# Attention and experts in fp32: products apart, sin from PSUM, other slots for the projections

## The chip, the cores and the metric

The kernel runs on one core of a Trainium2 chip. The metric is the device time of one execution in microseconds (us). A core has five engines that run their own instruction streams and meet through semaphores: TensorE (PE, with its weight loads shown apart as PEld), VectorE (DVE), ScalarE (ACT), GpSimd (POOL) and SyncE (SP), which here mostly issues DMA transfers. All arithmetic is fp32. SBUF holds tiles with 128 partitions; matmuls write to PSUM, from which DVE and ACT read.

## The reference

The input x is 4 batches x 1024 tokens x 256. Two layers follow one another, each with a residual and a layer norm:

```python
# attention, per batch: 16 heads of 64
proj = x @ W_in.T + b_in                  # q, k, v
q = rope(q, sin, cos); k = rope(k, sin, cos)
att = softmax(causal(q @ k.T / sqrt(64)))
x1 = layernorm(x + (att @ v) @ W_out.T + b_out)
# experts, 4096 tokens, 16 experts, the best 3 per token
gate = top3(softmax(x1 @ gate_w)); gate /= sum(gate)
x2 = layernorm(x1 + sum_e gate_e * (relu(x1 @ W1_e + b1_e) @ W2_e + b2_e))
```

with

```python
def _rope(x, sin, cos):
    d = x.shape[-1] // 2
    x_hi, x_lo = (x[..., :d], x[..., d:])
    y_lo = x_lo * cos + x_hi * sin
    y_hi = x_hi * cos - x_lo * sin
    return jnp.concatenate([y_lo, y_hi], axis=-1)
```

So a rotated tile is (tile x sin) + (tile with its halves swapped x cos), with the signs in the tables.

## The kernel before

**Pairs and slots.** Two heads of 64 fill the 128 partitions. The attention is a loop over 4 x 8 = 32 such pairs n (L428); b is the batch and p the pair in it. The 1024 queries of a pair are 8 chunks of 128. A pair has six slots k (L432) that take the chunks 7, 6, 5, 4, then 3 and 2 together, then 1 and 0 together. Chunk qc needs the (qc+1) x 128 keys up to the diagonal.

**What a slot does.** `scores` (L279) runs the score matmuls of the slot's chunks, at most 512 keys at a time, for both heads (L300). DVE adds the mask, copies the scores (negated by the factor of Q, -1/8) to SBUF and takes the running minimum in one instruction (L308, tile `nmax`), ACT takes the exponential and its sum (L320), `divide` (L331) forms the reciprocal on DVE (L334, `rinv`) and multiplies on POOL (L337). Two slots later `turn` (L346) transposes the probabilities P in blocks of 32 x 32 on DVE (L357), into `t_first` for the key half h = 0 (keys 0 to 511) and `t_last` for h = 1. `product` (L364) of key chunk j multiplies the turned P with the values `vr` on PE, 32 small matmuls on 32 x 64 array tiles (L378; the profile counts 64 instructions) into four PSUM tiles `y_ps`. It runs j = 7 first, j = 0 last; `close` (L386) then copies the four tiles to `yT` on ACT, and `out` (L397) multiplies `yT` with the output weights (L400, tile `oo`), a quarter in each of four slots; DVE adds it to the sum of the batch (L455, `acc`).

**Feeding the next pairs.** `project` (L200) makes half of Q or K of pair n+1: four matmuls into PSUM (L214, `pp`), an eviction on ACT with bias, and the scale for Q (L218). Once a tile of Q (512 wide) or K (1024 wide) is whole, four DMAs on SP copy it with its 32-row halves swapped (L230, `swq`, `swk`). `rotate` (L232) multiplies the tile in place by sin (L236; Q on DVE, K on POOL), the swapped copy by cos on POOL (L242), and adds on POOL (L245). `values` (L247) makes a quarter of V for two pairs at once (L254, `vv`), sends it to DRAM (`v_d`), and `spread` (L271) reads it back in the layout that the products need (`vr`).

**What sets the order.** PE runs in program order (L427). The other engines' order is set by a scheduler, to which `after(i, kind)` (L327) says that instruction i is issued after the last one of that kind. Matmul results of scores, projections, values and `out` share four PSUM buffers of the pool `ps_s`, the products four of `ps_y`. In slots k = 0 to 5 PE's order before is, with S, P, O, J, V for scores, product, out, projection and values:

| slot | before |
|---|---|
| 0 | S7, P4, O, J(K0) |
| 1 | S6, P3, P2, J(K1) |
| 2 | P1, P0, S5, J(Q1) |
| 3 | S4, P7, O, J(Q0) |
| 4 | S3, S2, P6, O, V |
| 5 | S1, S0, P5, O, V |

P4 to P0 belong to the pair before, P7 to P5 to the pair itself; J to the next pair. K is rotated at slot 2, Q1 (the queries 512 to 1023, which S7 to S4 need) at slot 3, Q0 at slot 5.

**Extra work in some pairs.** When a batch is done, its layer norm and router run among the pairs of the next batch: steps on DVE and PE in the slots 3 and 5 of pair p = 1, 1 and 3 of p = 2, the places of the entries at slot 3 of p = 3, and four indirect scatters on POOL (L673) in the slots 1 and 3 of p = 4, 5 and 6. In p = 7 POOL adds the output bias twice (L179, `residual`). The pairs p = 1, 2, 3 are called R1, R2, R3 below, those with scatters scatter pairs, and those without either plain. The experts come after the last pair.

Of the kernel before, what the change touches and what calls it, by code (L numbers as in the profile page):

```python
# [29 lines left out]
FP = mybir.dt.float32  # L30
# [7 lines left out]
P = 128  # L38
# [50 lines left out]
def attention(  # L89
# [5 lines left out]
    with ExitStack() as ctx:  # L95
# [54 lines left out]
        bq_s = cp.tile([P, NP], FP, tag="bq_s")  # L150
# [8 lines left out]
        nc.vector.tensor_scalar_mul(bq_s, bqk[:, 0, :], SCALE)  # L159
        mask = cp.tile([P, 512], FP, tag="mask")  # L160
        nc.gpsimd.memset(mask[:, : 512 - P], 0.0)
        make_causal_mask(nc, mask[:, 512 - P :], BIG)
# [35 lines left out]
        swps = {}  # L198

        def project(n, i, g):  # L200

            b, p = divmod(n, NP)
            if i == 0:
                res = rot[n, 0, g] = qkp.tile([P, 512], FP, tag=f"rotq{g}", name="rotq")
                half, whole = res, True
            else:
                whole = (n, 1) in rot
                if not whole:
                    rot[n, 1] = qkp.tile([P, T], FP, tag="rotk", name="rotk")
                res = rot[n, 1]  # L210
                half = res[:, ts(g, 512)]
            ps = ps_s.tile([P, 512], FP, tag="s", name="pp")
            for c in range(DC):
                nc.tensor.matmul(  # L214
                    ps, lhsT=wqk[n][:, c, i, :], rhs=xts[b, g][:, c, :],
                    start=(c == 0), stop=(c == DC - 1),
                )
            nc.scalar.activation(  # L218
                half, ps, AF.Identity,
                bias=(bq_s if i == 0 else bqk[:, 1, :])[:, p : p + 1],  # L220
                scale=SCALE if i == 0 else 1.0,
            )
            if whole:

                if i == 0:
                    swp = swps[n, 0, g] = qkp.tile([P, 512], FP, tag="swq", name="swq")
                else:
                    swp = swps[n, 1] = qkp.tile([P, T], FP, tag="swk", name="swk", bufs=1)
                for r in range(4):
                    nc.sync.dma_start(out=swp[ts(r, 32), :], in_=res[ts(r ^ 1, 32), :])  # L230

        def rotate(n, i, g=None):  # L232
            key = (n, i) if i else (n, i, g)
            swp, res = swps.pop(key), rot[key]
            at = slice(None) if i else ts(g, 512)
            first = (nc.gpsimd if i and n else nc.vector).tensor_tensor(  # L236
                res, res, sin[:, at], ALU.mult
            )
            if n:
                after(first, "divide" if i else "turn" if "turn" in order else "scores")  # L240
            eng = nc.vector if n == 0 and i else nc.gpsimd
            second = eng.tensor_tensor(swp, swp, cos[:, at], ALU.mult)  # L242
            if n:
                after(second, "divide")
            eng.tensor_tensor(res, res, swp, ALU.add)  # L245

        def values(n, cc):  # L247

            b = n // NP
            v = vp.tile([P, 2, 2, P], FP, tag="v", name="v")  # L250
            ps = ps_s.tile([P, 2, 2 * P], FP, tag="s", name="vv")
            for u in range(2):
                for c in range(DC):
                    nc.tensor.matmul(  # L254
                        ps[:, u, :],
                        lhsT=xts[b, cc // 2][:, c, ts(cc % 2 * 2 + u, P)], rhs=wv[n][:, c, :],
                        start=(c == 0), stop=(c == DC - 1),
                    )
            nc.scalar.copy(v.rearrange("p i u d -> p u i d"), ps.rearrange("p u (i d) -> p u i d", i=2))
            if cc == 0:  # L260
                vds[n // 2] = v_d.tile([NG, 2, 32, 2, 4, 2 * P], FP, tag="v_d", name="v_d")

            for i in range(2):
                nc.sync.dma_start(
                    out=vds[n // 2][cc // 2, i, :, cc % 2].rearrange("q k d -> k q d"),
                    in_=v[:, i],
                )
# [11 lines left out]
        def scores(n, qcs):  # L279
# [25 lines left out]
            for qc, hh, k0, n_k, s in parts:  # L305
                last = k0 + n_k == (qc + 1) * P
                m = sp.tile([P, 1], FP, tag=f"nmax{hh}", name="nmax")
                order["scores"] = nc.vector.tensor_tensor_reduce(  # L308
                    out=probs[n, qc, hh][:, ds(k0, n_k)], in0=s[:, :n_k],
                    in1=mask[:, 512 - n_k :] if last else zero[:, :n_k], scale=1.0,  # L310
# [3 lines left out]
                nmax[qc, hh] = m  # L314
                if last:
# [15 lines left out]
        def divide(n, ends, kind):  # L331
            for qc, rsum in ends:
                rinv = sp.tile([P, 2], FP, tag="rinv", name="rinv")
                after(nc.vector.reciprocal(rinv, rsum), kind)  # L334
# [11 lines left out]
        def turn(n, i, hh, kind):  # L346
# [5 lines left out]
            pr = probs.pop((n, i, hh))  # L352
            for h, (t, step) in enumerate(zip(turned[n], (7, 3))):
                n_j = min(4, i + 1 - 4 * h)
                if n_j <= 0:
                    continue
                order["turn"] = router.on_dve = after(nc.vector.transpose(  # L357
                    t[:, hh, :, ds(i - 4 * h, n_j, step=step), :],
                    pr[:, ds(512 * h, n_j * P)].rearrange("p (j u q) -> p u j q", u=4, q=32),
                ), kind)  # L360
# [48 lines left out]

        chunks = [(7,), (6,), (5,), (4,), (3, 2), (1, 0)]  # L410
        n_slots = len(chunks)
        n_pairs = B * NP
        for i, g in ((1, 0), (0, 0), (1, 1), (0, 1)):
            project(0, i, g)
        for cc in range(4):
            values(0, cc)
        rotate(0, 1)
        for g in (1, 0):
            rotate(0, 0, g)
# [7 lines left out]
        with tc.manual_schedule(engines={mybir.EngineType.PE}):  # L427
            for n in range(n_pairs + 2):  # L428
# [3 lines left out]
                for k in range(n_slots):  # L432
                    m, js = (n - 1, ((4,), (3, 2), (1, 0))[k]) if k < 3 else (n, (10 - k,))
                    if k == 2 and one_of(m):
                        for j in js:
                            product(m, j)
                        close(m)

                    ends = scores(n, chunks[k]) if one_of(n) else []
                    if k != 2 and one_of(m):  # L440
                        for j in js:
                            product(m, j)
                    part = None
                    if k in (0, 3, 4, 5) and one_of(n - 1 - (k == 0)):
                        part = out(n - 1 - (k == 0), (k - 3) % 4 if k else 3)
                    m, kk = divmod(n * n_slots + k - 2, n_slots)
                    last = "scores"
                    for hh in range(2):
                        if one_of(m):
                            for qc in chunks[kk]:  # L450
                                turn(m, qc, hh, last)
                            last = "turn"
                        if hh == 0 and part:
# [15 lines left out]
                    if one_of(n + 1):  # L469
                        if k < 4:  # L470
                            project(n + 1, *((1, 0), (1, 1), (0, 1), (0, 0))[k])
                        if k == 2:
                            rotate(n + 1, 1)
                        elif k in (3, 5):
                            rotate(n + 1, 0, int(k == 3))
                    m = n + 2 - n % 2
                    if k in (4, 5) and one_of(m):
                        values(m, 2 * (n % 2) + k - 4)
# [627 lines left out]
```

## Time and profile before

| | |
|---|---|
| median of 14 runs | 1807.1 us (1800.67 to 1810.48) |
| profiled execution | 1811.8 us, span 1809.9 |
| attention | to about 1345 us |
| busy share of the span PE, DVE, ACT, POOL | 89%, 64%, 39%, 66% |
| mean granted clock of PE | 0.96 of full speed |
| waits of PE for `nmax` at `oo` | 31.6 us, 24 times |
| waits of PE for `t_last` at products | 19.3 us, 11 times |
| waits of PE for the router's `x2T` | 17.6 us, 3 times |
| idle of PE ahead of products put down to "issue" | 14.3 us, 20 times |

A line of a timeline gives start, duration, engine, line of the code, operation, output and inputs, how many instructions it joins, and in brackets how long the engine was idle before and what ended that. A line of the list of waits gives who waited for whom, the total in us, how many times, and the longest. A line of a table of stretches gives the stretch, its length, the busy time of PE, PEld, DVE, ACT and POOL with the number of instructions, the granted clock as a fraction of full speed, the share of the DMA engines and their GB/s.

### The profile page before, as it was taken

How to read it: one execution, taken by the hardware profiler on the slowest of the kernel's cores; microseconds unless marked ns; L12 is line 12 of the kernel's file. 1: busy time of each engine (PE TensorE's matmuls, PEld its weight loads, DVE VectorE, ACT ScalarE, POOL GpSimd, SP SyncE). 2: the span in 40 equal slices, each digit the busy share in tenths (PEclk: the TensorE clock that was granted, in tenths of full speed). 3: DMA queues.
4: the chain of work that ended last, by engine and by line, in shares of the span. 5: the costliest groups of instructions: out<-in, count | busy, mean ns of one | idle time of the engine just before them, and what ended most of it. 6: DMA issues, size and time to landing. Idle time of an engine off the chain costs nothing.

```text
span 1809.9 us, 51958 instructions
## 1 busy us (share of the span) xinstructions
PE 1606.1 (89%) x20920; PEld 1120.3 (62%) x20920; DVE 1164.3 (64%) x3458; ACT 713.2 (39%) x1634; POOL 1192.0 (66%) x1077
## 2 busy tenths in 40 slices
PE   7899999988999899888999988898889999999980
PEld 3556555655555555555555555555568888888870
DVE  4588778877877679687877868867846222222224
ACT  3445444444444445343444544344422222222214
POOL 3777657755578856556888555577766778888542
PEclk9899999999999999999999989999899999999995
DMA  6364644564355545435455463343467989998747
GB/s 182 96 161 121 147 111 112 132 182 105 92 124 121 121 111 162 125 91 122 121 123 124 111 191 92 91 109 94 114 254 199 208 242 246 241 241 240 212 87 279
DMA packets 118167, 272.97 MB, mean 151 GB/s; under 512 B 21873, under 2 KB 72433, under 8 KB 102562
## 3 DMA queue, kind: packets, MB, share of 16 engines
q1 hardware_dynamic: 93122, 239.91, 48.5%
q0 software_dynamic: 24656, 29.68, 9.0%
q8 instruction: 167, 2.74, 0.7%
q14 instruction: 78, 0.64, 0.1%
q10 hardware_dynamic: 144, 0.01, 0.0%
HBM read 183.17 MB, written 52.79 MB: 130 GB/s over the span
## 4 chain that ended last, share of the span: by engine, by line
PE 59%; DVE 16%; DMA 9%; issue 8%; SPq 4%; ACT 3%; POOL 1%; ACTq 0%; DVEq 0%; POOLq 0%
PE y_ps L378 14%; PE ps L874 11%; PE ps L890 10%; PE s L300 8%; PE pp L214 6%; PE oo L400 4%; DVE p L308 4%; PE vv L254 4%; DMA swq<-rotq 3%; SPq L230 3%; DVE t_first L357 3%; DVE t_last L357 2%; ACT p L320 2%; DMA xT<-in_xT_dram 1%; PE ps L862 1%
## 5 line engine op out<-in xcount | busy, mean ns | idle before, releaser
L337 POOL TENSOR_SCALAR p<-p,rinv 128x512 f32<-128x512 f32 (+7 forms) x512 | 385.8, 769 | 405.8 <-DVE rinv L334 401.7
L320 ACT ACTIVATE p<-p,nmax 128x512 f32<-128x512 f32 (+7 forms) x512 | 392.0, 766 | 470.9 <-DVE nmax L308 411.7
L300 PE MATMUL s<-rotk,rotq 64*128 64x512 f32 (+3 forms) x1536 | 336.7, 522 | 46.0 <-DVE x2T L578 17.6
L300 PEld LDWEIGHTS s<-rotk,rotq 64*128 64x128 f32 x1536 | 158.5, 189 | 229.3 <-issue 96.6
L308 DVE CUSTOM_DVE_ANT_0 p<-s,zero 128x512 f32<-128x512 f32 x256 | 165.7, 684 | 206.1 <-PE s L300 206.1
L357 DVE STREAM_TRANSPOSE t_first<-p 128x512 f32<-128x512 f32 (+3 forms) x512 | 289.0, 588 | 1.0 <-POOL p L337 0.9
L214 PE MATMUL pp<-xT,wqk 128*128 128x512 f32 x512 | 253.2, 619 | 19.6 <-DVE nmax L308 10.6
L904 POOL DMA_INDIRECT sums<-y,ids x112 | 178.9, 1597 | 69.4 <-DVE y L900 38.5
L378 PE MATMUL y_ps<-t_first,vr 32*64 32x160 f32 (+3 forms) x8192 | 208.4, 339 | 13.6 <-issue 12.3
L879 ACT ACTIVATE hid<-ps,w 128x256 f32<-128x256 f32 x224 | 94.1, 471 | 314.4 <-issue 252.1
L895 DVE TENSOR_TENSOR y<-ps,w 128x512 f32<-128x512 f32 x56 | 38.7, 692 | 275.7 <-PE ps L890 275.7
L378 PEld LDWEIGHTS y_ps<-t_first,vr 32*64 32x64 f32 x8192 | 169.3, 131 | 66.2 <-issue 37.4
L874 PE MATMUL ps<-xg,w 128*128 128x256 f32 x896 | 204.4, 382 | 2.6 <-DVE xg L864 2.6
L890 PE MATMUL ps<-w,hid 128*128 128x256 f32 x896 | 202.6, 379 | 0.0
L890 PEld LDWEIGHTS ps<-w,hid 128*128 128x128 f32 x896 | 169.8, 190 | 23.0
L400 PE MATMUL oo<-wo,yT 128*128 128x256 f32 x512 | 153.0, 425 | 32.9 <-DVE nmax L308 31.6
L874 PEld LDWEIGHTS ps<-xg,w 128*128 128x128 f32 x896 | 167.1, 191 | 23.7 <-DVE xg L864 2.8
L378 PE MATMUL y_ps<-t_last,vr 32*64 32x96 f32 (+3 forms) x7424 | 146.3, 255 | 31.8 <-DVE t_last L357 19.3
L378 PEld LDWEIGHTS y_ps<-t_last,vr 32*64 32x64 f32 x7424 | 115.6, 135 | 92.9 <-issue 46.2
L214 PEld LDWEIGHTS pp<-xT,wqk 128*128 128x128 f32 x512 | 93.9, 194 | 111.4 <-issue 69.7
L308 DVE CUSTOM_DVE_ANT_0 p<-s,mask,nmax 128x512 f32<-128x512 f32 (+3 forms) x256 | 130.3, 545 | 0.8 <-issue 0.4
L400 PEld LDWEIGHTS oo<-wo,yT 128*128 128x128 f32 x512 | 91.6, 199 | 56.1 <-DVE nmax L308 35.2
(150 smaller groups left out, 2011.6 us busy)
## 6 DMA issues: line engine op xcount, KB each, us to landing
vr<-v_d SPq DMA_DIRECT2D x256, 256.0 KB
w<-in_wall_dram SPq DMA_DIRECT2D x56, 1154.0 KB
swq<-rotq SPq DMA_DIRECT2D x256, 64.0 KB
swk<-rotk SPq DMA_DIRECT2D x128, 128.0 KB
v_d<-v SPq DMA_DIRECT2D x128, 128.0 KB
wqk<-in_w_qk_dram SPq DMA_DIRECT2D x32, 256.0 KB
xT<-in_xT_dram SPq DMA_DIRECT2D x8, 512.0 KB
wv<-in_w_v_dram SPq DMA_DIRECT2D x16, 256.0 KB
```

The source lines that it names most:

```text
L214: nc.tensor.matmul(ps, lhsT=wqk[n][:, c, i, :], rhs=xts[b, g][:, c, :], start=(c == 0), stop=(c == DC - 1),)
L300: nc.tensor.matmul(s[:, :n_k], lhsT=rot[n, 0, qc // 4][ts(hh, KD), ts(qc % 4, P)], rhs=k[ts(hh, KD), ds(k0, n_k)], start=True, stop=True,)
L308: order["scores"] = nc.vector.tensor_tensor_reduce(out=probs[n, qc, hh][:, ds(k0, n_k)], in0=s[:, :n_k], in1=mask[:, 512 - n_k :] if last ...
L320: nc.scalar.activation(pr, pr, AF.Exp, bias=m, scale=-1.0, accum_out=rsum[:, hh : hh + 1])
L337: order["divide"] = router.behind = nc.gpsimd.tensor_scalar(pr, pr, rinv[:, hh : hh + 1], 1.0, ALU.mult, ALU.mult)
L357: order["turn"] = router.on_dve = after(nc.vector.transpose(t[:, hh, :, ds(i - 4 * h, n_j, step=step), :], pr[:, ds(512 * h, n_j * P)].rea ...
L378: nc.tensor.matmul(st[n][a][ts(hh, KD), ds(32 * j, 32 * (TC - j))], lhsT=vrs[n, h][ts(a, 32), jh // 2 * 8 + 2 * u + jh % 2, ts(hh, KD)], r ...
L400: nc.tensor.matmul(ps[:, v, :], lhsT=st[n][:, ts(2 * h + v, P)], rhs=wo[n], start=True, stop=True,)
L874: nc.tensor.matmul(ps[:, f - f0, :], lhsT=w[:, ds(c * FF + f * P, P)], rhs=xg[:, c, :], start=(c == 0), stop=(c == DC - 1),)
L879: nc.scalar.activation(hid[:, f, :], ps[:, f - f0, :], AF.Relu, bias=w[:, ds(B1_AT + f, 1)])
L890: nc.tensor.matmul(ps[:, h, :], lhsT=hid[:, f, ts(h, P)], rhs=w[:, ds(W2_AT + f * D, D)], start=(f == 0), stop=(f == FC - 1),)
L904: s = behind(nc.gpsimd.indirect_dma_start(out=sums[t % 2], out_offset=bass.IndirectOffsetOnAxis(ap=ids[:, h, i : i + 1], axis=0), in_=y[:, ...
```

## The change

- PE's order in the slots, and with it what is projected where: a product of one chunk is never followed at once by that of another.

| slot | after |
|---|---|
| 0 | S7, P4, O, J(K0), P3 |
| 1 | S6, P2, J(K1) |
| 2 | P1, S5, P0, J(Q1) |
| 3 | S4, P7, O, V |
| 4 | S3, S2, P6, O, V |
| 5 | S1, S0, P5, O, J(Q0) |

- A projection is read twice from PSUM: ACT writes it with the bias to a raw tile (`rawq`, `rawk`), from which the swap's DMAs read; DVE adds the bias and multiplies by sin in one instruction and writes the tile that is to be rotated, issued after the reciprocal of the slot ("inverse"). `rotate` is left with cos and the add, on POOL behind the divides: K at slot 2, Q1 at slot 4, Q0 at slot 0 of its own pair.
- The scale -1/8 moves from the projection of Q to the reduction of the scores; the mask's constant is divided by it.
- The turns of a slot are ordered by key half: h = 1 of both heads, the sum of `oo`, then h = 0.
- Values take the slots 3 and 4 (4 and 5 before).
- At the start: the order of projections is K0, K1, Q1, Q0, the rotations come ahead of the values, and only the quarters 2 and 3 of V are made; the quarters 0 and 1 follow in the slots 1 and 2 of pair 0.

```diff
         def project(n, i, g):
             if i == 0:
-                res = rot[n, 0, g] = qkp.tile([P, 512], FP, tag=f"rotq{g}", name="rotq")
-                half, whole = res, True
+                half = rot[n, 0, g] = qkp.tile([P, 512], FP, tag=f"rotq{g}", name="rotq")
+                part = raw = qkp.tile([P, 512], FP, tag="rawq", name="rawq")
+                whole = True
...
-            nc.scalar.activation(
-                half, ps, AF.Identity,
-                bias=(bq_s if i == 0 else bqk[:, 1, :])[:, p : p + 1],
-                scale=SCALE if i == 0 else 1.0,
-            )
+            bias = bqk[:, i, p : p + 1]
+            nc.scalar.activation(part, ps, AF.Identity, bias=bias)
+            m = nc.vector.scalar_tensor_tensor(
+                half, ps, bias, sin[:, ts(g, 512)], ALU.add, ALU.mult
+            )
+            if n:
+                after(m, "inverse")
...
-                    nc.sync.dma_start(out=swp[ts(r, 32), :], in_=res[ts(r ^ 1, 32), :])
+                    nc.sync.dma_start(out=swp[ts(r, 32), :], in_=raw[ts(r ^ 1, 32), :])

         def rotate(n, i, g=None):
             key = (n, i) if i else (n, i, g)
             swp, res = swps.pop(key), rot[key]
-            at = slice(None) if i else ts(g, 512)
-            first = (nc.gpsimd if i and n else nc.vector).tensor_tensor(
-                res, res, sin[:, at], ALU.mult
+            eng = nc.vector if n == 0 and i else nc.gpsimd
+            first = eng.tensor_tensor(
+                swp, swp, cos if i else cos[:, ts(g, 512)], ALU.mult
             )
-            if n:
-                after(first, "divide" if i else "turn" if "turn" in order else "scores")
-            eng = nc.vector if n == 0 and i else nc.gpsimd
-            second = eng.tensor_tensor(swp, swp, cos[:, at], ALU.mult)
-            if n:
-                after(second, "divide")
+            if "divide" in order:
+                after(first, "divide")
             eng.tensor_tensor(res, res, swp, ALU.add)
...
-                    m, js = (n - 1, ((4,), (3, 2), (1, 0))[k]) if k < 3 else (n, (10 - k,))
-                    if k == 2 and one_of(m):
-                        for j in js:
-                            product(m, j)
-                        close(m)
-
-                    ends = scores(n, chunks[k]) if one_of(n) else []
-                    if k != 2 and one_of(m):
-                        for j in js:
-                            product(m, j)
-                    part = None
+                    here, before = one_of(n), one_of(n - 1)
+                    part, ends = None, []
+                    if k == 2 and before:
+                        product(n - 1, 1)
+                    if here:
+                        ends = scores(n, chunks[k])
+                    if k < 3 and before:
+                        product(n - 1, (4, 2, 0)[k])
+                        if k == 2:
+                            close(n - 1)
+                    if k >= 3 and here:
+                        product(n, 10 - k)
...
-                        if k < 4:
-                            project(n + 1, *((1, 0), (1, 1), (0, 1), (0, 0))[k])
+                        if k in (0, 1, 2, 5):
+                            project(n + 1, int(k < 2), int(k in (1, 2)))
                         if k == 2:
                             rotate(n + 1, 1)
-                        elif k in (3, 5):
-                            rotate(n + 1, 0, int(k == 3))
+                        elif k == 4:
+                            rotate(n + 1, 0, 1)
+                    if k == 0 and one_of(n):
+                        rotate(n, 0, 0)
+                    if k == 0 and before:
+                        product(n - 1, 3)
                     m = n + 2 - n % 2
-                    if k in (4, 5) and one_of(m):
-                        values(m, 2 * (n % 2) + k - 4)
+                    if k in (3, 4) and one_of(m):
+                        values(m, 2 * (n % 2) + k - 3)
+                    if k in (1, 2) and n == 0:
+                        values(0, k - 1)
```

## The prediction

> **What bounds the kernel now.** I read the page's busy times first, then a table of stretches (the start, the pairs of the attention without extra work, those with the router, the experts), then the list of waits inside each stretch, and last the timeline around the longest waits.
>
> ```profile
> PE 1606.1 (89%) x20920; PEld 1120.3 (62%) x20920; DVE 1164.3 (64%) x3458; ACT 713.2 (39%) x1634; POOL 1192.0 (66%) x1077
> ```
>
> TensorE is the bound on average, at 89%. The change can touch only the attention: 32 head pairs, up to 1345 us; the experts behind them keep their 464.9 us. Between the first slot-3 products of successive pairs I read the period of each pair: 43.4 us for the first, 37.5 us in the mean over 12 plain pairs (36.66 at best), 47.3 to 48.4, 44.1 to 45.3 and 46.2 to 46.7 for the three router pairs of a batch (R1, R2, R3), 39.2 in the mean over eight with scatters. The next rows are seven plain pairs and one batch's router pairs (length, then busy time of PE, PEld, DVE, ACT, POOL, granted clock):
>
> ```profile
> 85.89:347.15 261.26, 244.11 (x4089) 154.57 (x4088) 209.16 (x607) 127.22 (x294) 175.73 (x164) 1.00 0.53 129
> 384.97:523.22 138.25, 121.47 (x1806) 78.32 (x1805) 102.79 (x317) 56.24 (x129) 78.31 (x74) 0.93 0.47 120
> ```
>
> A plain pair has (261.26 - 244.11)/7 = 2.45 us in which PE is idle (3.1 us longer than its segments at their shortest, summed below); a router pair 5.6 us, at a lower clock. What PE waits for in those seven plain pairs:
>
> ```profile
> PE oo L400 <- DVE nmax L308: 9.9, 7, 1.4
> PE s L300 <- ACT rotq L218: 2.6, 7, 0.4
> PE pp L214 <- DVE nmax L308: 2.5, 7, 0.4
> ```
>
> The first, 1.4 us in each pair, has a visible cause: on DVE the sin multiply sits ahead of the reductions that free PSUM for `oo`.
>
> ```profile
> 648.05 2.63 DVE L236 TENSOR_TENSOR rotq<-rotq,sin 128x512 f32<-128x512 f32 x1
> 650.60 0.68 DVE L308 CUSTOM_DVE_ANT_0 p<-s,mask 128x512 f32<-128x512 f32 x1
> ```
> ```profile
> 651.34 1.13 PE L400 MATMUL oo<-wo,yT 128*128 128x256 f32 x4 [1.45 <-DVE nmax L308]
> ```
>
> In R1 pairs the same multiply waits for the swap's DMAs, which read the tile that it overwrites, and PE waits 5.4 to 6.5 us behind it, then runs slowly:
>
> ```profile
> 395.09 0.71 DVE L236 TENSOR_TENSOR rotq<-rotq,sin 128x512 f32<-128x512 f32 x1 [5.81 <-DMA swq<-rotq]
> ```
> ```profile
> 396.45 1.64 PE L300 MATMUL s<-rotk,rotq 64*128 64x384 f32 x2 [5.39 <-DVE x2T L578]
> ```
>
> Whole-kernel waits that the change also speaks to:
>
> ```profile
> PE s L300 <- DVE x2T L578: 17.6, 3, 6.5
> PE y_ps L378 <- issue: 14.3, 20, 2.0
> PE s L300 <- POOL rotq L245: 8.9, 2, 4.8
> ```
>
> "issue" means that PE waited for nothing the profile shows. The longest such gap stands behind two products back to back, and half clock follows it (a projection takes 1.81 to 1.91 us otherwise):
>
> ```profile
> 625.82 2.67 PE L378 MATMUL y_ps<-t_first,vr 32*64 32x160 f32 x128
> 630.95 3.56 PE L214 MATMUL pp<-xT,wqk 128*128 128x512 f32 x4 [2.46 <-issue]
> ```
>
> **The change part by part: prices.** The rows of the operations that move:
>
> ```profile
> L236 DVE TENSOR_TENSOR rotq<-rotq,sin x64: 667/1072/2631, 15.9 to 1282.7; 128x512 f32<-128x512 f32 x64
> L236 POOL TENSOR_TENSOR rotk<-rotk,sin x31: 2343/2369/2382, 47.0 to 1268.3; 128x1024 f32<-128x1024 f32 x31
> L242 POOL TENSOR_TENSOR swq<-swq,cos x64: 1256/1271/1777, 15.9 to 1288.8; 128x512 f32<-128x512 f32 x64
> L245 POOL TENSOR_TENSOR rotq<-rotq,swq x64: 1260/1277/1396, 17.8 to 1290.2; 128x512 f32<-128x512 f32 x64
> L455 DVE TENSOR_TENSOR acc<-oo,acc x128: 644/654/692, 88.4 to 1333.3; 128x512 f32<-128x512 f32 x128
> ```
>
> *Sin.* Two DVE multiplies a pair (mean 1.49 us) and one on POOL (2.37) go; four DVE multiplies come that read PSUM. Before has none with these operands. Low end: L455's 0.65 us, also one PSUM and one SBUF source, never over 0.69 beside POOL. High end: today's 1.49. I take 0.66, since PSUM is what L455 shares: DVE 4 x 0.66 - 2 x 1.49 = -0.3 us a pair, POOL -2.4. The L236 row spreads by four from shortest to longest beside POOL's two-input operations, L455's does not. [...]
>
> *Queues.* The swap DMAs (8 of Q and 4 of K a pair, same bytes) now read raw tiles, so no multiply waits for them; POOL's cos multiply does, two slots later (Q0: the next pair). Values and v_d/vr DMAs go one slot earlier on SP, ahead of Q0's swaps, which then have until slot 4 of the next pair. ACT's evictions are the same four (0.68 us). The scale in the reduction, the mask and the order of the 512 turns cost nothing: same instructions, and a turn is read two slots after it is made; without that cover one late turn costs PE up to 0.7 us. A projection's PSUM buffer is now released by DVE, behind the reciprocal: between 0 and 4 x 0.66 us a pair. I take 0: the following PSUM user comes later than 0.66 us after the eviction.
>
> **A plain pair, walked slot by slot** with PE's shortest segment times in the trace (S and P with a number are the scores and the product of that chunk, O = out 0.97, J = projection 1.81 to 1.91, V = values 1.82):
> - slot 0: S7 1.92, P4 1.14, O, J, P3 1.14 = 6.98
> - slot 1: S6 1.70, P2 1.46, J = 5.07
> - slot 2: P1 1.56, S5 1.50, P0 1.86, J = 6.83
> - slot 3: S4 1.28, P7 0.67, O, V = 4.74, and about 0.65 of waiting for ACT (its exponentials and four yT copies stand ahead of the raw eviction); ends at 24.3
> - slot 4: S3,2 1.70, P6 0.84, O, V = 5.33
> - slot 5: S1,0 0.86, P5 0.97, O, J = 4.71
>
> That is 34.3 us. But the next S7 needs Q1 rotated, and this now stands on POOL behind slot 4's divides: from S3,2's start 5.81 us to the reciprocal (as in the pair at 643.8), 0.23 to POOL, four divides 2.6 (2 x 0.72 + 2 x 0.59), cos 1.27, add 1.28, some 0.14 between = 11.33, against PE's 10.04. So S7 waits 1.3 us, and a plain pair takes 35.6 us, 1.9 less than 37.5. I use 1.75, since the shortest pair of before already has 36.66.
>
> **Sum against the profiled 1811.8 us** (span 1809.9; 0.26% above the median of 1807.1):
> - 9 plain pairs x 1.75: -16
> - 3 pairs with a residual: the 2.5 us add lies between cos and add of Q1; 38.2 against 37.7: +1.5
> - 8 scatter pairs: four scatters (5.2 us) lie ahead of the add; 38.8 against 39.2: -3
> - 3 R1 pairs: the 5.4 to 6.5 us wait and slow clock behind it. At least 5.4 each, at most the 10 us over a plain pair; 7.5 taken: -22
> - 6 R2 and R3 pairs: 6 to 8 us of router work stand on DVE ahead of slot 4's reciprocal; before, S7 started 17.05 and 17.2 us after slot 4 did, by the walk 17.9 and 18.8; the vanished gaps give that back. 0, bounds -18 and +10.
> - Start: with Q1 rotated before the values, the first scores move from 25.5 to 21.6 and pair 1's from 63.3 to 54 (the 4.1 and 4.8 us waits for POOL's L245 and half clock behind them): -9
>
> Together -48.5: 1763 profiled, 1758 beside the median. R3's part leans on 2.46 us of idling being followed by half clock. [...]
>
> **Rivals.**
> 1. *POOL becomes the bound (slower).* Q1's rotation is the one transfer of work that lands behind a longer chain. For: L242's row reaches 1.78 us, and POOL's divides wait up to 10.2 us for a reciprocal. Against: POOL has 2.4 us less to do. The 48.5 us are 1.67 us for each of the 29 pairs listed: once the add ends later than 11.33 + 1.67 = 13.0 us after S3,2's start, the kernel is slower. One more operation like the residual's 2.3 us in between gives 29 x 2.3 - 48.5 = +18: 1825.
> 2. *PSUM held by the DVE multiplies.* All four exposed: 4 x 0.66 x 30 = +79, 1837; a third of that, 1784. For: four buffers only. Against: the walk's 0.
> 3. *R1 pairs give nothing*: POOL's cos waits for the swap's DMAs in DVE's place (before has such a wait of 13.3 us), and S7 behind it: 1758 + 22 = 1780.
> 4. *The issue gaps stay*, because they come from something else than two adjacent products: +14, 1772.
> 5. *Better than the walk*: Q1 not late; 1.3 x 20 pairs and R2/R3's 18: -44, 1714.
> 6. *The change does not do what it says*: the PSUM form takes 1.49 us too. Then 4 x (1.49 - 0.66) = 3.3 us more a pair stand on DVE ahead of reductions; if 1.4 of them reach PE, as today at `oo`, 1.4 x 30 = +42: 1800.
>
> **How the numbers follow.** My forecast (1735 to 1772, the walk to within 0.5 us a pair) gets 0.50; better (rival 5) 0.12; rivals 3, 4 and 6 and the smaller share of rival 2 (1772 to 1803) 0.20; what ends within 0.2% (3.6 us, about what a measurement of this kernel can tell from no change) 0.04; slower (rival 1, the rest of 2) 0.14. The range 1718 to 1803 holds the first three but for some 0.04.
>
> **What would show it.** Right: `oo` no longer waits for `nmax` in plain pairs; the new multiplies at 0.66 us; no wait of scores for x2T; no gap over 1 us behind products; plain periods near 35.6 with a wait of S7 for POOL's rotq add of some 1.3 us. Wrong: that last wait over 3 us, projections or `oo` waiting for the new multiply, or POOL waiting for the swaps in R1 pairs with PE idle behind.

## The result, and the profile after

The changed kernel takes 1822.2 us in the median of 10 runs, beside 1807.6 us for the kernel before: 1.0079 of its time, with a 95% interval of 1.0064 to 1.0093. So it is slower, by 0.8%. The forecast was 1758 us, in a range from 1718 to 1803. The profiled executions took 1817.3 us after and 1811.8 before; they stand 5.5 us apart where the medians stand 14.6 apart, since one profile lies at the lower end of its kernel's runs and the other at the upper end. The sums below account for the 5.5 us between the profiles.

The busy times of the engines, from the page of the kernel after:

```profile
PE 1620.1 (89%) x20920; PEld 1113.7 (61%) x20920; DVE 1174.8 (65%) x3520; ACT 707.4 (39%) x1634; POOL 1097.9 (60%) x1046
```

POOL is busy 94 us less, 73 of which were its K multiply, and that bought nothing. The next list is what PE waited for in the six plain pairs at the start of the kernel after (80.9 to 309.0 us), one wait of each kind in nearly every pair:

```profile
PE s L299 <- DVE rotq L221: 6.7, 6, 1.1
PE s L299 <- POOL rotq L244: 5.7, 6, 1.0
PE pp L215 <- DMA wqk<-in_w_qk_dram: 2.7, 4, 1.0
```

The wait of `oo` for `nmax` (1.4 us a pair before) is gone, as is "issue", and three others have come. Over the whole kernel they are:

```profile
PE s L299 <- POOL rotq L244: 68.9, 28, 6.3
PE s L299 <- DVE rotq L221: 32.0, 30, 1.1
PE pp L215 <- DVE nmax L307: 10.4, 4, 3.6
PE pp L215 <- DMA wqk<-in_w_qk_dram: 10.1, 8, 5.3
```

Before, scores waited 8.9 us for POOL's rotq, twice.

The first of the plain waits, on the timelines of one pair of the kernel after. DVE's multiply from PSUM (line 221) begins only when ACT's eviction of the same PSUM tile (line 220) has ended, here and at every projection (none of the 128 sooner than 0.03 us behind it), and ACT's eviction of Q1 stands behind four yT copies. In order: DVE, ACT, PE.

```profile
232.33 0.75 DVE L221 SCALAR_TENSOR_TENSOR rotq<-pp,bqk,sin 128x512 f32<-128x512 f32 x1 [1.25 <-ACT rawq L220]
```
```profile
230.18 1.54 ACT L390 ACTIVATE yT<-y_ps,bv 128x256 f32<-128x256 f32 x4
231.60 0.69 ACT L220 ACTIVATE rawq<-pp,bqk 128x512 f32<-128x512 f32 x1
```
```profile
233.14 0.48 PE L299 MATMUL s<-rotk,rotq 64*128 64x128 f32 x2 [1.12 <-DVE rotq L221]
```

231.60 + 0.69 = 232.29, and DVE starts at 232.33. The buffer is free at 233.08, 233.14 is S4's last pair of matmuls. S4's second half takes 1.92 us from start to start of what follows, 1.60 more than its 0.32 undisturbed.

The second wait, on POOL and PE of the same pair: Q1's rotation follows slot 4's four divides, and S7 waits for its add.

```profile
205.35 2.49 POOL L339 TENSOR_SCALAR p<-p,rinv 128x512 f32<-128x512 f32 x4 [3.74 <-DVE rinv L336]
207.79 1.27 POOL L239 TENSOR_TENSOR swq<-swq,cos 128x512 f32<-128x512 f32 x1
209.14 1.27 POOL L244 TENSOR_TENSOR rotq<-rotq,swq 128x512 f32<-128x512 f32 x1
```
```profile
210.46 1.99 PE L299 MATMUL s<-rotk,rotq 64*128 64x512 f32 x8 [0.92 <-POOL rotq L244]
```

S3,2 had started at 199.31, so the add ended 11.10 us later; the walk had 11.33. Where POOL has more to do, this wait is 3.2 us (the residual pair at 325.8) and 5.3 us (R2 at 453.6), and S7 behind it runs at half clock: it takes 3.56 and 4.10 us from start to start rather than 1.92, at a granted clock of 0.53 and 0.50.

The third place is the pair in which the layer norm of a batch is made. Its eight multiplies now stand on DVE ahead of S6's reductions, beside POOL's cos and add, and slot 1's projection waits for a PSUM buffer:

```profile
373.09 4.65 DVE L83 TENSOR_SCALAR acc<-acc,mv,rstd 128x256 f32<-128x256 f32 x8
```
```profile
378.40 1.98 PE L215 MATMUL pp<-xT,wqk 128*128 128x512 f32 x4 [3.47 <-DVE nmax L307]
```

In the kernel before they stood behind the reductions and took 2.7 us, and the pair took 37.8 us, beside 37.4 for a plain one.

### The profile page after: what moved, and what is told of

Same layout as the page of the kernel before. It is cut to its first block, busy times and chain, and to the rows that moved or that the text cites. A ratio compares the mean times of both kernels' runs of the same rounds, so it can differ in the third digit from the quotient of the medians.

```text
span 1815.4 us, 51884 instructions
## 1 busy us (share of the span) xinstructions
PE 1620.1 (89%) x20920; PEld 1113.7 (61%) x20920; DVE 1174.8 (65%) x3520; ACT 707.4 (39%) x1634; POOL 1097.9 (60%) x1046
## 4 chain that ended last, share of the span: by engine, by line
PE 58%; POOL 11%; DVE 9%; DMA 8%; ACT 7%; issue 6%; SPq 1%; ACTq 0%; POOLq 0%; DVEq 0%
PE ps L882 11%; PE s L299 10%; PE ps L898 10%; PE y_ps L377 9%; PE pp L215 6%; PE oo L399 4%; PE vv L253 4%; POOL p L339 4%; DMA wqk<-in_w_qk_dram 4%; ACT p L322 3%; ACT yT L390 2%; DVE p L307 2%; POOL table L681 2%; POOL rotq L244 1%; POOL swq L239 1%
## 5 line engine op out<-in xcount | busy, mean ns | idle before, releaser
L339 POOL TENSOR_SCALAR p<-p,rinv 128x512 f32<-128x512 f32 (+7 forms) x512 | 375.4, 750 | 508.8 <-DVE rinv L336 500.9
L299 PE MATMUL s<-rotk,rotq 64*128 64x512 f32 (+3 forms) x1536 | 342.1, 540 | 106.0 <-POOL rotq L244 68.9
L356 DVE STREAM_TRANSPOSE t_first<-p 128x512 f32<-128x512 f32 (+3 forms) x512 | 275.6, 580 | 0.6 <-POOL p L339 0.5
L377 PE MATMUL y_ps<-t_first,vr 32*64 32x160 f32 (+1 forms) x8192 | 218.4, 343 | 3.0 <-DVE t_first L356 2.7
L912 POOL DMA_INDIRECT sums<-y,ids x112 | 178.7, 1596 | 68.4 <-DVE y L908 36.7
L903 DVE TENSOR_TENSOR y<-ps,w 128x512 f32<-128x512 f32 x56 | 38.7, 692 | 274.4 <-PE ps L898 274.4
L377 PEld LDWEIGHTS y_ps<-t_first,vr 32*64 32x64 f32 x8192 | 162.3, 132 | 85.1 <-DVE t_first L356 32.1
L882 PEld LDWEIGHTS ps<-xg,w 128*128 128x128 f32 x896 | 167.1, 191 | 24.7 <-DVE xg L872 3.9
L377 PE MATMUL y_ps<-t_last,vr 32*64 32x96 f32 (+3 forms) x7424 | 140.4, 257 | 3.0 <-issue 0.8
L253 PE MATMUL vv<-wv,xT 128*128 128x256 f32 x512 | 135.0, 411 | 0.0
```

The costliest lines, as they stand in the source:

```text
L253: nc.tensor.matmul(ps[:, u, :], lhsT=xts[b, cc // 2][:, c, ts(cc % 2 * 2 + u, P)], rhs=wv[n][:, c, :], start=(c == 0), stop=(c == DC - 1),)
L299: nc.tensor.matmul(s[:, :n_k], lhsT=rot[n, 0, qc // 4][ts(hh, KD), ts(qc % 4, P)], rhs=k[ts(hh, KD), ds(k0, n_k)], start=True, stop=True,)
L339: order["divide"] = router.behind = nc.gpsimd.tensor_scalar(pr, pr, rinv[:, hh : hh + 1], 1.0, ALU.mult, ALU.mult)
L356: order["turn"] = router.on_dve = after(nc.vector.transpose(turned[n][h][:, hh, :, ds(i - 4 * h, n_j, step=7 - 4 * h), :], probs[n, i, hh] ...
L377: nc.tensor.matmul(st[n][a][ts(hh, KD), ds(32 * j, 32 * (TC - j))], lhsT=vrs[n, h][ts(a, 32), jh // 2 * 8 + 2 * u + jh % 2, ts(hh, KD)], r ...
L882: nc.tensor.matmul(ps[:, f - f0, :], lhsT=w[:, ds(c * FF + f * P, P)], rhs=xg[:, c, :], start=(c == 0), stop=(c == DC - 1),)
```

## The experiments

**How they are read.** All periods below are the mean time from one P7 to the next in the profile of a kernel, over the same groups of pairs: the first six plain ones, three with a residual in slot 4, three with the layer norm, three each of R1, R2, R3, eight scatter pairs. "Ratio" is to the kernel before on the same chip, with its 95% interval.

| kernel | ratio | plain | residual | norm | R1 | R2 | R3 | scatter |
|---|---|---|---|---|---|---|---|---|
| before | 1 | 37.4 | 37.6 | 37.8 | 47.7 | 44.7 | 46.5 | 39.2 |
| b_prod | 0.9858 (0.9836 to 0.9880) | 36.1 | 35.5 | 38.9 | 44.1 | 44.2 | 44.3 | 37.9 |
| b_turn2 | 0.9786 (0.9758 to 0.9814) | 35.4 | 35.0 | 39.5 | 42.1 | 43.1 | 41.7 | 39.7 |
| a_slots2 | 0.9787 (0.9752 to 0.9821) | 37.2 | 36.9 | 40.3 | 39.5 | 42.4 | 41.2 | 37.9 |
| a_rot3 | 0.9889 (0.9860 to 0.9917) | 37.7 | 37.0 | 42.0 | 39.9 | 48.5 | 41.8 | 38.8 |
| after | 1.0079 (1.0064 to 1.0093) | 38.0 | 41.6 | 42.7 | 39.8 | 47.7 | 44.9 | 38.8 |
| a_three | 0.9655 (0.9625 to 0.9686) | 36.3 | 35.9 | 41.1 | 38.7 | 45.9 | 40.9 | 36.7 |
| a_norm2 | 0.9584 (0.9559 to 0.9610) | 36.5 | 35.8 | 36.2 | 38.7 | 45.7 | 40.8 | 36.8 |
| b_best | 0.9598 (0.9571 to 0.9625) | 35.4 | 34.9 | 35.7 | 40.7 | 43.3 | 41.6 | 37.8 |

The rows from before to after are a ladder, each with one more part of the change: products, turns, sin from PSUM (with the scale in the reduction and the new order of projections at the start), the new slots but for Q1's rotation, and that rotation.

**a_rot3: Q1's rotation back in slot 3.**

```diff
-                        elif k == 4:
+                        elif k == 3:
                             rotate(n + 1, 0, 1)
```

> The changed kernel, with Q1's rotation (cos and add on POOL) one slot earlier: behind slot 3's divides and ahead of slot 4's, where the kernel before has it. Theory A (the loss comes from several waits in series, of which PE's 68.9 us for POOL's rotq add is the largest): these waits fall under 5 us, the half clock that follows the long ones goes as well, and the kernel takes 1735 to 1760 us. Rival B (PSUM and DVE set the pace of a pair, and POOL is only the last to arrive): the wait is replaced by another one at the same place, 1800 us or more.

It took 1786.1 us beside 1806.7: between the two theories. PE's waits after the edit:

```profile
PE s L299 <- DVE rotq L221: 33.8, 33, 1.1
PE pp L215 <- DMA wqk<-in_w_qk_dram: 18.7, 16, 5.3
...
PE s L299 <- POOL rotq L244: 6.7, 2, 3.4
```

The 68.9 us went to 6.7, and the kernel gained 1.9% (1.0079 to 0.9889), some 34 us. Not all of it: in plain pairs the period fell only from 38.0 to 37.7, because S7's last weight load now waits for the PSUM buffer of Q0's projection, which the new slots put right ahead of S7 (2.69 us from start to start where 1.92 is undisturbed); over the whole kernel the projections also wait longer for `wqk` (18.7 us, 10.1 in the changed kernel). Rival B is right there, theory A in the residual pairs (41.6 to 37.0) and in R3. R2 gains nothing (47.7 to 48.5): S7 no longer waits 5.3 us for POOL, but 2.1 us for reductions; what takes up the rest is not shown.

**a_close: the raw eviction of Q1 ahead of the yT copies.**

```diff
-            nc.scalar.activation(part, ps, AF.Identity, bias=bias)
+            order["raw"] = nc.scalar.activation(part, ps, AF.Identity, bias=bias)
...
-                nc.scalar.activation(
+                after(nc.scalar.activation(
                     yT[:, :, a, :], y[:, : 2 * P].rearrange("p (i q) -> p i q", q=32),
                     AF.Identity, bias=bv[:, p : p + 1],
-                )
+                ), "raw")
```

(`close` is called behind `project` in slot 2.)

> The changed kernel, with the raw eviction of Q1 ahead of the four yT copies on ACT. Theory A: the last two score matmuls of S4 wait for the PSUM buffer of Q1's projection, which DVE frees only after ACT has read it, and ACT reads it 1.5 us late because of the yT copies. PE's 32.0 us for L221 go to under 6 us, S4's second half takes 0.3 to 0.5 us in place of 1.9, and as Q1's rotation counts from slot 4's start nothing takes that back: 1.4 x 30 = 42 us less, about 1780 us. Rival B: the pair is bound by POOL, S7 waits longer by what S4 waits less, and the time stays within 1815 to 1825 us.

It took 1787.6 us, 0.9906 (0.9881 to 0.9931).

```profile
PE s L299 <- POOL rotq L244: 72.3, 28, 5.9
...
PE s L299 <- DVE rotq L221: 8.7, 30, 0.3
```

The wait for line 221 went from 32.0 to 8.7 us, and the one for POOL took back almost none of it (68.9 to 72.3). Theory A holds, at 31 rather than 42 us: the two waits are in series, and 23 us less of the one are not taken back by the other.

**a_three: both, and the weights three slots earlier.**

```diff
-                    if k == 5 and one_of(n + 2):
+                    if k == 2 and one_of(n + 2):
                         late(load_qk(n + 2))
```

> The two edits together, and the weights wqk of the pair after next loaded in slot 2 rather than in slot 5. Theory A: the gains add up (75 for Q1, 42 for S4, 8 for wqk): 1690 to 1715 us, below both kernels, with plain pairs near 34.5 us. Rival B: no more than the better of the two edits alone.

It took 1742.4 us, 0.9655 (0.9625 to 0.9686). That is 77 us less than the changed kernel (1.0079 - 0.9655 of 1807), where the two edits alone were worth 34 and 31: they add up, as theory A says, though each is smaller than it had them. The other 12 us came with the weights, whose edit was not run alone. Layer norm pairs stay at 41.1 us. In six successive pairs of it (118 to 333 us, 35.8 to 36.5 us each) PE's list has little but 0.3 us a pair at S4; what the projection's buffer still costs lies at S7, where the weight loads (PEld) show it:

```profile
PE s L299 <- DVE rotq L221: 1.7, 6, 0.3
```
```profile
169.20 0.29 PEld L299 LDWEIGHTS s<-rotk,rotq 64*128 64x128 f32 x2 [0.48 <-DVE rotq L221]
```

**b_prod: the order of products alone, in the kernel before.**

```diff
-                    if k == 2 and one_of(m):
-                        for j in js:
-                            product(m, j)
-                        close(m)
-
-                    ends = scores(n, chunks[k]) if one_of(n) else []
+                    if k == 2 and before:
+                        product(n - 1, 1)
+                    if here:
+                        ends = scores(n, chunks[k])
+                    if k < 3 and before:
+                        product(n - 1, (4, 2, 0)[k])
+                        if k == 2:
+                            close(n - 1)
...
                             rotate(n + 1, 0, int(k == 3))
+                    if k == 0 and before:
+                        product(n - 1, 3)
```

> The kernel before with nothing but the new order of products on PE (P3 behind slot 0's projection, P2 alone in slot 1, S5 between P1 and P0). Theory A: the idle time ahead of products and projections that was put down to issue (16.8 us) falls below 2 us, with some of the half clock behind it; against that the projection of slot 1 has 1.1 us less between it and S6, so waits for nmax grow in the pairs with the layer norm (some 4 us in each of three): 1785 to 1805 us. Rival C (the gaps come from something else than two adjacent products): they stay, and the kernel takes 1805 us or more.

It took 1779.5 us, 27 us less than before and better than theory A's range. The gaps put down to "issue" ahead of products and projections fell from 16.8 to 4.2 us, and the layer norm pairs did lose 1.1 us. What theory A did not have is the plain pairs: most of these took 35.4 us, and PE's list for six successive pairs has one entry.

```profile
PE s L300 <- ACT rotq L218: 2.0, 6, 0.3
```

The 1.4 us at `oo` are gone although the sin multiply is still there, still on DVE, and still two SBUF operands beside POOL. S5 no longer stands behind two products, so DVE idles 2.48 us ahead of S5's reductions rather than 5.63 (the fourth block is the kernel before), and what follows from them is earlier: the divides, and K's rotation behind them on POOL. In order: DVE and POOL in slot 4, POOL and DVE in the kernel before, and PE.

```profile
191.04 0.69 DVE L308 CUSTOM_DVE_ANT_0 p<-s,zero 128x512 f32<-128x512 f32 x1 [2.48 <-PE s L300]
...
201.15 1.54 DVE L236 TENSOR_TENSOR rotq<-rotq,sin 128x512 f32<-128x512 f32 x1 [0.16 <-DMA swq<-rotq]
202.62 0.68 DVE L308 CUSTOM_DVE_ANT_0 p<-s,mask 128x512 f32<-128x512 f32 x1
```
```profile
199.78 2.37 POOL L242 TENSOR_TENSOR swk<-swk,cos 128x1024 f32<-128x1024 f32 x1
```
```profile
647.78 2.35 POOL L242 TENSOR_TENSOR swk<-swk,cos 128x1024 f32<-128x1024 f32 x1
```
```profile
230.29 0.69 DVE L308 CUSTOM_DVE_ANT_0 p<-s,zero 128x512 f32<-128x512 f32 x1 [5.63 <-PE s L300]
```
```profile
203.35 1.13 PE L400 MATMUL oo<-wo,yT 128*128 128x256 f32 x4
```

The multiply that the prediction shows ran from 648.05 to 650.68 us, and POOL's cos multiply of K to 650.13; here they end at 202.69 and 202.15. In the kernel before, the multiply of Q1 ends 0.55 us after POOL's in all 27 pairs outside R1 (the first pair left out), whether it lasts 1.81 or 2.63 us, and here, where it lasts 1.54, 0.54 us after it: its end goes by POOL's. So the new order acts through POOL. From P7's start the multiply ends after 6.85 us in the plain pairs of the kernel before and after 5.40 here, and `oo` no longer waits.

**b_turn, a_slots, a_sbuf, a_norm.** These four ran on another chip, on which the kernel before took 1896.4 us; its scatter pairs and what follows the last pair were slower (41 to 46 us a scatter pair in a_norm, 36 to 37 in the same kernel run again), so their ratios are not set beside the others. Three of them were run again, below.

b_turn adds the new order of turns to b_prod (the same lines as in the change).

> The kernel before with the new order of products and the new order of turns, and nothing else (the second rung of a ladder from before to after; the first, products alone, took 1779.5 us). Theory A: turns of the late key half come 0.5 to 1.2 us earlier, which shortens PE's waits for t_last at products in the router pairs (14.0 us on the first rung) and costs nothing elsewhere: 1765 to 1780 us. Rival: the early key half now comes later and waits for t_first (8.6 us) grow by as much: 1780 to 1790.

It took 1827.2 us there, 0.9666 (0.9599 to 0.9734), with most plain pairs at 34.8 us (35.1 in the mean); in that profile `t_last` is waited for 4.1 us and `t_first` 3.3, where b_prod had 14.0 and 8.6. Theory A's mechanism shows; the times are taken from b_turn2.

a_slots is the changed kernel with projections, rotations and values in the slots of before; at the start all four quarters of V follow the rotations:

```diff
-                        if k in (0, 1, 2, 5):
-                            project(n + 1, int(k < 2), int(k in (1, 2)))
+                        if k < 4:
+                            project(n + 1, *((1, 0), (1, 1), (0, 1), (0, 0))[k])
                         if k == 2:
                             rotate(n + 1, 1)
-                        elif k == 4:
-                            rotate(n + 1, 0, 1)
-                    if k == 0 and one_of(n):
-                        rotate(n, 0, 0)
+                        elif k in (3, 5):
+                            rotate(n + 1, 0, int(k == 3))
...
-                    if k in (3, 4) and one_of(m):
-                        values(m, 2 * (n % 2) + k - 3)
+                    if k in (4, 5) and one_of(m):
+                        values(m, 2 * (n % 2) + k - 4)
```

> The changed kernel with projections, rotations and values in the slots of the kernel before (the third rung: products, turns, and sin from PSUM). Theory A: the wait of R1 pairs for x2T (7.8 us on the first rung) goes and DVE's multiply no longer reaches 2.6 us, but the PSUM buffer of a projection is freed only after ACT's and then DVE's pass over it; S4's second half waits 1.0 us longer in each pair (+30 us): 1785 to 1805 us. Rival B (sin from PSUM is a gain in itself, and only the new slots lose): 1750 to 1770 us.

1857.2 us there, 0.9797 (0.9727 to 0.9867): 1.3% over b_turn on that chip. That went theory A's way and did not last: see a_slots2.

a_sbuf lets DVE multiply the raw tile instead of PSUM:

```diff
-                half, ps, bias, sin[:, ts(g, 512)], ALU.add, ALU.mult
+                half, part, 1.0, sin[:, ts(g, 512)], ALU.mult, ALU.mult
```

> The changed kernel, with DVE's multiply reading the raw tile from SBUF in place of PSUM, so that ACT alone frees the projection's buffer. Theory A: PE's 32.0 us for L221 at S4 shrink to some 10 (0.3 us each, for ACT), 0.75 x 30 = 23 us less, against which the multiply has two SBUF sources again and takes 0.7 to 2.6 us; 1795 to 1815 us. Rival: the multiply from SBUF delays the reductions as it did in the kernel before, and oo or pp wait for nmax by over 1 us in each pair: 1825 us or more.

1904.4 us, 1.0056 (1.0023 to 1.0088): slower than the kernel before, as the changed kernel is. Both mechanisms of the expectation showed at once, and the ratio, some 1817 us where the kernel before takes 1807, lies between their two ranges.

```profile
PE oo L399 <- DVE nmax L307: 21.0, 30, 1.7
...
PE s L299 <- ACT rawq L220: 7.1, 21, 0.4
```

S4 waited 7.1 us (for ACT alone) instead of 32.0: from its start to that of P7 it takes 2.10 us in plain pairs, 2.88 in the changed kernel, 2.13 in the kernel before. And `oo` waited 21.0 us for reductions behind a multiply of up to 2.35 us, where it did not in the changed kernel. One wait takes the place of the other: plain pairs take 37.8 us in its profile, 38.0 in that of the changed kernel. Which of the two forms is cheaper in these slots was not measured on one chip.

a_norm is a_three with the layer norm's multiplies held back:

```diff
-        nc.vector.tensor_scalar(
+        hook(nc.vector.tensor_scalar(
...
-            layernorm(nc, small, accs[b], 0, TC, eps_t)
+            layernorm(
+                nc, small, accs[b], 0, TC, eps_t,
+                (lambda i: after(i, "turn")) if b < B - 1 else (lambda i: i),
+            )
```

> The kernel a_three (1742.4 us) with the eight multiplies of the layer norm held on DVE until the turns of slot 1, as the kernel before has them. Theory A: the 3.5 us that slot 1's projection waits for nmax in the three pairs with a layer norm go, with the half clock behind them: periods of 37 in place of 41.1 us there, 10 to 13 us less, 1729 to 1733 us. Rival: the normalised rows and with them the router's steps come later and R1 or R2 pairs lose as much: 1742.

1846.5 us there, 0.9747 (0.9678 to 0.9816), with layer norm pairs at 36.3 us in the profile.

**The second time, on one chip** (1804.5 us for the kernel before).

> The kernel before with the new orders of products and of turns, once more, to stand beside the next three on one chip. In its profile of the first time plain pairs take 34.8 us, beside 37.5 before and 35.4 with the products alone. Theory A: 0.965 of the kernel before, which is 1740 to 1755 us where the kernel before takes 1807.

1764.1 us. The ratio of 0.9786 misses the 0.965, which came from the slow chip; it is 0.7% below b_prod.

> The rung that adds sin from PSUM, once more. In its profile of the first time plain pairs take 36.3 us or more, 1.5 over b_turn, with PE waiting 25.8 us for L221 at S4. Theory A: slower than b_turn by 1.0 to 1.8%. Rival B (sin from PSUM gains in itself): not slower than b_turn.

1762.6 us, equal to b_turn2: the expectation fails, and rival B is right that sin from PSUM does not cost in sum. The row of the table says why. Plain and residual pairs lose 1.8 to 1.9 us, with S4 waiting as in the changed kernel,

```profile
PE s L299 <- DVE rotq L221: 32.8, 31, 1.3
```

and the scores behind each projection of Q pay for DVE's pass: in a plain pair S4 takes 2.88 us up to P7 where b_turn2 has 2.10, and S3,2, behind Q0's projection in these slots, 2.47 where it has 1.70. R1 and scatter pairs gain 2.6 and 1.7.

> The changed kernel with Q1's rotation a slot earlier, raw Q1 ahead of the yT copies, the weights earlier, and the layer norm's multiplies behind slot 1's turns, once more. In its profile of the first time the three pairs with the layer norm take 36.2 to 36.4 us, where a_three has 41.1. Theory A: 0.957 to 0.960 of the kernel before, below the 0.9655 of a_three.

1728.4 us, 0.9584: as expected. Layer norm pairs took 36.2 us instead of 41.1.

b_best keeps from the sin part only the raw tile:

```diff
-                res = rot[n, 0, g] = qkp.tile([P, 512], FP, tag=f"rotq{g}", name="rotq")
+                rot[n, 0, g] = qkp.tile([P, 512], FP, tag=f"rotq{g}", name="rotq")
+                res = raws[n, 0, g] = qkp.tile([P, 512], FP, tag="rawq", name="rawq")
...
-                res, res, sin[:, at], ALU.mult
+                res, raws.pop(key), sin[:, at], ALU.mult
```

> b_turn with two things added: the projections go to a raw tile first, from which the swap reads and which the sin multiply reads from SBUF into the tile to be rotated (slots, engines and PSUM buffers as in the kernel before), and the layer norm's multiplies behind slot 1's turns. Theory A: what is worth having of the sin part is that no multiply waits for the swap's DMAs; R1 pairs fall from 44.4 to about 39 us, pairs with the layer norm from 38.7 to 36, together 20 to 25 us below b_turn, and this is the fastest of all. Rival: POOL waits for the swap in the multiply's place and S4 behind it, and R1 pairs stay at 44: only 8 us below b_turn.

1731.8 us, 32 us below b_turn2, but not the fastest: a_norm2 and it overlap. Layer norm pairs fell to 35.7 us, R1 pairs by 1.4 us only; the scatter pairs, which neither theory had, fell by 1.8 us each, 15 us together. Both beat the kernel before by 4%. What is left in b_best over 120 to 340 us is small:

```profile
PE s L305 <- ACT rawq L223: 2.3, 7, 0.3
PE pp L219 <- DMA wqk<-in_w_qk_dram: 2.1, 3, 0.8
```

## Why the prediction was wrong

The terms of its sum, beside the same groups in the two profiles:

| term | forecast, us | profiles, us |
|---|---|---|
| 9 pairs taken as plain | -16 | +3.7 for six plain ones, +14.5 for three with the layer norm |
| 3 with a residual | +1.5 | +12.2 |
| 8 scatter pairs | -3 | -3.5 |
| 3 R1 | -22 | -23.8 |
| 6 R2 and R3 | 0 (-18 to +10) | +8.9 for R2, -4.9 for R3 |
| start | -9 | -5.0 |
| from the last pair on | 0 | +3.3 |

They add to -48.5 and +5.4. R1 and the scatters were right in size. For R1 that is in part luck: the forecast put all of it down to the multiply that waits for the swap, and by the ladder an R1 pair falls by 3.7 us with the products, 1.9 with the turns, and only 2.6 with sin from PSUM, where no multiply waits for the swap any more.

**The walk of a plain pair** gave 35.6 us; the pair shown above took 37.7. Its segments are 0.67 us longer than the shortest of the trace (the products P4 to P0 by 0.44, P5 and P6 by 0.23): 0.30 of it are P1 and P3, whose shortest times stand ahead of another product (see the end). S4 waits 1.60 us, not 0.65: +0.95. `wqk` comes 0.82 us late: +0.82. POOL's chain was right, 11.10 for 11.33, and S7 waits 0.92 rather than 1.3 us: -0.38. 35.6 + 0.67 + 0.95 + 0.82 - 0.38 = 37.66.

**The step that failed** is "A projection's PSUM buffer is now released by DVE ... between 0 and 4 x 0.66 us a pair. I take 0". Rival 2 had the price. The walk counted ACT's delay but let DVE's pass cost nothing, as if ACT and DVE read PSUM side by side. In the trace none of the 128 multiplies starts before ACT has ended its pass over the same tile, DVE is idle for ACT's eviction ahead of 105 of them, 86.4 us in all, and the multiply takes 0.72 to 0.75 us. At S4 the runs show this price alone: up to P7 it takes 2.88 us in the changed kernel and 2.10 in a_sbuf, where DVE no longer reads the buffer, and it goes from 2.10 to 2.88 from b_turn2 to a_slots2. So the term is 0.78 us a pair at S4, about as long as the pass (in a_slots2 the same again at S3,2, and in a_rot3 at S7; in the changed kernel S7 waits for POOL there anyway); over 30 pairs that is an estimated 23 of the 54 us between the forecast and the profile. The rest of S4's 1.60 us is the wait for ACT.

```profile
L221 DVE SCALAR_TENSOR_TENSOR rotk<-pp,bqk,sin x64: 716/751/753, 9.5 to 1259.8; 128x512 f32<-128x512 f32 x64
L221 DVE SCALAR_TENSOR_TENSOR rotq<-pp,bqk,sin x64: 725/750/752, 12.9 to 1281.0; 128x512 f32<-128x512 f32 x64
```

What puts the two passes in this order is not shown. That they stand in series also makes the start of the first one count: a_close, which moves only ACT's pass up, gains 31 us.

**Layer norm pairs** were priced as plain, and lost 14.5 us rather than gaining 5: nothing in the walk asked where the layer norm's 2.7 us of DVE work would land once P3 no longer stood between S6 and slot 1's projection. It landed ahead of S6's reductions, where beside POOL's cos and add it took 4.65 us. a_norm2 shows this: held back, none of its multiplies takes over 0.49 us, and the pair goes from 41.1 to 36.2 us. Some 20 of the 54 us lie in these pairs, 11 in the residual ones; the three shares overlap, since these pairs have an S4 too.

**Rival 1** was the right one for sign and place, at 0.14. The forecast put its break-even at an add 1.67 us late in each pair; in plain pairs it was never late by that, but the residual pairs, with the add for the bias between cos and add, which the sum priced at +0.5 us a pair, lost 4.1, and R2 has 5.3 us of waiting with half clock behind it. a_rot3 is worth 34 us, of which little lies in plain pairs and none in R2.

**The wait at `oo`** did go, as forecast, and the cause that was named holds: a_sbuf puts the SBUF multiply back, and 21.0 us of it with it. But the prediction credited the gain to sin from PSUM, and b_prod has it without: with the new order of products POOL's cos multiply of K ends 1.45 us earlier in a plain pair, the sin multiply with it, and the reductions behind it are in time. The changed kernel removes the one wait twice. The price of the new multiply was nearly right (never over 0.75 beside POOL, for 0.66).

**The issue gaps** go with adjacent products here, so rival 4 is out: 14.3 us ahead of products became 0.8 in the kernel after, and 4.2 in b_prod, which changes only the order. Adjacent products are not the whole cause: on the slow chip gaps of the same name stand ahead of products and inside them in kernels that keep products apart (18.4 us in 44 gaps in b_turn and 37.4 in 67 in a_norm, where the same kernels have 3.4 and 2.0 us on the other chip). What PE lacks there was not tried.

**What the whole change is made of**, by the ladder: products -1.4%, turns -0.7%, sin from PSUM 0.0, the slots of Q0, values and start +1.0%, Q1's rotation behind slot 4's divides +1.9%. The steps are differences of ratios, each uncertain by some 0.4%.

## What to carry to other kernels

When an operation reads a PSUM tile that another engine reads too, look whether the two passes stand in series, as they do in all 128 projections here (0.69 and 0.75 us), and count both before the buffer is free; and look for what stands ahead of the first of them. Walk the pairs with extra work on their own: slack that a plain pair does not need is what hides a layer norm or a bias add. A change in several parts is worth taking apart on the chip: here two parts gained 2.1% and the slots lost 2.9%, and undoing four of the losses made the same change 4.2% faster than the kernel before.

## What the hardware showed unexpectedly

A product that has another one right behind it is some 0.15 us shorter from its start to that of what follows (P1 1.56 us at its shortest in the kernel before, the last pair left out, 1.70 in the kernel after; P3 1.14 and 1.30): a sum of shortest segments is not what a pair takes.

Eight 128x256 layer norm multiplies took 2.7 us behind the reductions in the kernel before, 4.65 us beside POOL's two-input operations in the kernel after, where the longest single one took 1.42 us against a median of 0.40. The six long ones, 0.97 to 1.42 us, all ran beside POOL's cos or add; no other took over 0.43.

The length of a gap alone did not decide whether half clock followed: behind 2.46 us of idling (kernel before, at 630.95) the granted clock was 0.55 for 3.6 us, behind 3.23 us (kernel after, at 325.8) 0.53 for 3.5 us, and behind 3.47 us (kernel after, at 378.40) it was 1.00.

The kernel before took 1896.4 us on one chip and 1804.5 to 1807.6 on the others. The same kernel, as b_turn there and as b_turn2, spans 1806.6 and 1759.4 us in its profiles, with plain pairs of the same length (35.1 and 35.4 us). Of the 47 us, 21 lie in the last pair's products on `t_first` (30.3 us from first to last for 9.0) and 13 in what follows it; scatter pairs are slower by 0.9 us. One product instruction on `t_first` takes as long on both (347 and 344 ns in the mean), but the 8192 of them keep PE busy for 260.2 us rather than 221.6, and PE's idle time put down to "issue" is 24.7 us rather than 4.6. What held it up was not tried.
